# Bringing a largest value and a count to all partitions: through DRAM and VectorE, or through TensorE

## The chip, the cores and the metric

The kernel runs on one core of a Trainium2 chip. The core has TensorE (PE, matrix products and transposes into PSUM), VectorE (DVE), ScalarE (ACT), GpSimd (POOL) and SyncE (SP), which here only issues transfers. Each engine works through its own list of instructions in order; an instruction that waits holds up all that stand behind it on its engine. The metric is the device time of one execution in microseconds (us), the median of several runs.

## The reference

Two layers over x of 2 x 512 rows of 512 numbers, each an attention-like part and a feed-forward part, each followed by a layer norm. What matters here is the feed-forward part of the first layer:

```python
def _L0_ffn_ref(x, w_gate, w_up, w_down):
    xf = x / 128.0
    gate = einsum('bsh,ih->bsi', xf, w_gate)
    up = einsum('bsh,ih->bsi', xf, w_up)
    inter = silu(gate) * up
    inter_q = trunc(clip(inter * 128.0, -128.0, 127.0))
    down = einsum('bsi,hi->bsh', inter_q, w_down)
    return trunc(clip(down * 128.0, -128.0, 127.0))
```

The weights that the inputs bring are ternary: each is -s, 0 or s, with one s for each of the three matrices. The gate and up matrices are 1376 x 512, down is 512 x 1376.

## The kernel before

**Ternary weights found at run time.** The kernel doesn't take it for granted that the weights are ternary. It takes the largest weight of a first block as s, divides every weight by s, multiplies back and counts the places where the product differs from the weight. Where the count is zero, the products run on the divided weights in fp32r (a faster matmul form); if not, a branch takes the plain fp32 weights. This is done twice: "up" for gate and up together (two scales, 22 blocks to check), and "down" (one scale, 11 blocks).

A largest value or a count comes out of DVE as one number on each of 128 partitions. All partitions then need the largest over the 128, or the sum over the 128. Before the change TensorE does this:

- `over_partitions` (L180): PE transposes mx (128 x k) into PSUM as pmx (k x 128), DVE takes the maximum along the row (top) and puts it on the diagonal of a k x k tile (dg).
- `scales` (L191): PE multiplies a block of ones with dg, which gives the k values on all partitions (pbc); DVE limits them to sc and takes the reciprocal inv.
- `verdict` (L213): PE multiplies a 128 x 128 block of ones with the counts tot, so that every partition has the sum (pf); DVE turns it into yes and no, the flag (an integer on one partition, which PE reads for its branch) and eff, the scale that later steps use.

That makes six small steps on PE: pmx, pbc and pf, each for up and for down.

**Stages.** In the first stage (up to about 72 us) PE computes the queries of eight heads for each of two halves b of the rows (`queries`, L352; tiles pq). ACT takes two functions of each (e and r), and DVE joins them (q). In the turn of the second half, weight products are folded into mw (`fold`, L385: a product pmw on PE, col and mw on ACT), and `largest` (L172) takes mx_up from the first chunk of gate and up weights, gus[0]. In the turns of later heads `check_up` (L439) checks blocks: ACT divides (t, L433), DVE compares and counts (junk, L204). In the second stage (72 to 131 us) PE multiplies the queries with mw (`read`, L392; tiles po), eight row tiles after one another; ACT and DVE take the results out of PSUM, POOL adds. The last checks, the total and the verdict of up lie in this stage, and `divided` (L506) makes the divided weights tu. In the third stage (131 to 210 us) `up` (L560) runs 22 groups of products pg and pu under the branch. Beside it run mx_down, the checks of the down weights (POOL divides into td at L435, DVE compares), the total of down and its verdict (L702 to L708). The products of down (pd, L622) follow, under the second branch, and then the second layer.

**Loads and order.** SP issues nearly all loads in one queue: x and the query weights, then `wo` (16 of 512 KB, the last of which wait for free buffers), gus[0] in front of the last four, then ten more gu chunks and the small weights of the second layer (L309 to L315). The down weights wait for the room of the first stage's tiles. The gate and up weights of the second layer (L744) go into the buffers of the first layer's chunks, and each waits for the last product that reads the old chunk. A scheduler orders each engine's instructions except POOL's by the order of the program and by when it reckons that their operands are ready; `tc.issue_after(ins)` sets an instruction behind `ins` on the same engine.

Of the kernel before, what the change touches and what calls it, by code (L numbers as in the profile page):

```python
# [10 lines left out]
F32 = mybir.dt.float32  # L11
# [25 lines left out]
def kernel(  # L37
# [19 lines left out]
    nc = tc.nc  # L57
# [5 lines left out]
    xp = ctx.enter_context(tc.tile_pool(name="xp", bufs=8))  # L63
    xtp = ctx.enter_context(tc.tile_pool(name="xtp", bufs=2))
    small = ctx.enter_context(tc.tile_pool(name="small", bufs=4))
    ps = ctx.enter_context(tc.tile_pool(name="ps", bufs=8, space=PSUM))

# [11 lines left out]
    def psum(name):  # L79
        return ps.tile([P, 512], F32, tag="mm", name=name)  # L80
# [91 lines left out]
    def largest(blocks, name):  # L172

        k = len(blocks)
        mx = small.tile([P, k], F32, tag=f"mx{k}", name=f"mx_{name}", bufs=1)
        for i, w in enumerate(blocks):
            nc.vector.reduce_max(mx[:, i : i + 1], w, AX.X)
        return mx

    def over_partitions(mx, name):  # L180

        k = mx.shape[-1]
        pm = psum(f"pmx_{name}")
        nc.tensor.transpose(pm[:k, :P], mx, ident)
        top = small.tile([k, 1], F32, tag=f"top{k}", name=f"top_{name}", bufs=1)
        nc.vector.reduce_max(top, pm[:k, :P], AX.X)
        dg = small.tile([k, k], F32, tag=f"dg{k}", name=f"dg_{name}", bufs=1)
        nc.vector.tensor_scalar_mul(dg, ident[:k, :k], top)
        return dg

    def scales(dg, name):  # L191

        k = dg.shape[-1]
        pb = psum(f"pbc_{name}")
        nc.tensor.matmul(pb[:, :k], ones[:k, :], dg, start=True, stop=True)
        sc = const.tile([P, k], F32, tag=f"sc_{name}", name=f"sc_{name}")
        nc.vector.tensor_scalar(sc, pb[:, :k], 1e-30, 3e38, ALU.max, ALU.min)
        inv = const.tile([P, k], F32, tag=f"inv_{name}", name=f"inv_{name}")
        nc.vector.reciprocal(inv, sc)  # L199
        return sc, inv  # L200
# [7 lines left out]
    def total(counts, name):  # L208
        tot = small.tile([P, 1], F32, tag="tot", name=f"tot_{name}", bufs=1)
        nc.vector.reduce_sum(tot, counts, AX.X)  # L210
        return tot

    def verdict(tot, sc, name):  # L213

        k = sc.shape[-1]
        pf = psum(f"pf_{name}")
        nc.tensor.matmul(pf[:, :1], ones, tot, start=True, stop=True)
        yes = small.tile([P, 1], F32, tag="yes", name=f"yes_{name}", bufs=1)
        nc.vector.tensor_scalar(yes, pf[:, :1], 0.0, None, ALU.is_equal)
        no = small.tile([P, 1], F32, tag="no", name=f"no_{name}", bufs=1)  # L220
        nc.vector.tensor_scalar(no, pf[:, :1], 0.0, None, ALU.not_equal)
# [9 lines left out]
    def up_weights(gu_in, name, chunks=range(len(CHUNKS))):  # L231
        gus = []
        for c in chunks:
            i, n = CHUNKS[c]
            gu = wffn.tile([P, 2, NK, n], F32, tag=f"gu{c}", name=f"gu{name}_{c}")
            at = 2 * HID * i
            nc.sync.dma_start(
                gu.rearrange("p a k i -> p (a k i)"),
                gu_in[at : at + 2 * HID * n].rearrange("(p f) -> p f", p=P),
            )  # L240
            gus.append(gu)
        return gus
# [38 lines left out]
    with tc.tile_pool(name="a0w", bufs=1) as a0w, tc.tile_pool(name="a0", bufs=2) as a0:  # L281
# [24 lines left out]
                halves.append(w)  # L306
            wos.append(halves)

        gus += up_weights(gu0_in, "0", range(1, len(CHUNKS)))  # L309
        nc.sync.dma_start(wqkv, wqkv_in.rearrange("(k p) f -> p k f", p=P))  # L310
        bqk = const.tile([D, 3], F32, tag="bqk", name="bqk")
        nc.sync.dma_start(bqk, bqk_in)
        nc.sync.dma_start(bv, bv_in.to_broadcast([P, D]))
        nc.sync.dma_start(wo1, wo1_in)
        nc.sync.dma_start(bo, bo_in.to_broadcast([P, HID]))  # L315

# [24 lines left out]
        def first_queries(pq, xt):  # L341
# [7 lines left out]
                    done = query_products(pq, xt, 0, ts(t, P))  # L349
            return done  # L350

        def queries(b, xt, h):  # L352
# [8 lines left out]
            nc.scalar.activation(e, pq, AF.Exp, bias=bq[:, h : h + 1])  # L361
            r = a0.tile([D, S], F32, tag="r", name=f"r_{b}_{h}")
            nc.scalar.activation(r, pq, AF.Relu, bias=bq[:, h : h + 1])
            q = a0.tile([D, S], F32, tag="q", name=f"q_{b}_{h}", bufs=16)
            nc.vector.scalar_tensor_tensor(q, e, 1.0, r, ALU.min, ALU.add)
            qs[b].append(q)
            return done

# [97 lines left out]
        for h in range(NH):  # L466
            queries(1, xt1, h)
            if h == 0:
                sum_weights(nc.vector, 4)
                sum_weights(nc.gpsimd, 5)  # L470
                fold(0)
                fold(1)
                mx_up = largest(
                    [gus[0][:, a].rearrange("p k i -> p (k i)") for a in range(2)], "up"
                )
            elif h == 1:
                top_up = over_partitions(mx_up, "up")
            elif h == 2:
                sc_up, inv_up = scales(top_up, "up")
                fold(2)  # L480
                fold(3)
                sum_weights(nc.vector, 6)
                sum_weights(nc.gpsimd, 7)
            elif h == 3:
                fold(4)
            elif h == 5:
                fold(5)
                fold(6)
            elif h == 6:
                fold(7)  # L490
            if h >= 3:
                for _ in range(3):
                    check_up(*checks.pop(0))
        order = [(b, t) for b in range(B) for t in range(NT)]
        def norm_a0(i, steps):

# [19 lines left out]
        for i, (b, t) in enumerate(order):  # L516
            steps = read(b, t, lambda steps: norm_a0(i - 1, steps) if i else None)
            for _ in range((3, 2, 2, 0, 0, 0, 0, 0)[i]):
                check_up(*checks.pop(0))
            if i == 3:  # L520
                tot_up = total(counts, "up")
            elif i == 4:
                flag_up, eff_up = verdict(tot_up, sc_up, "up")
            if i in (3, 4, 5):
                for a in range(2):
                    divided(i - 3, a)
            if i == 5:
# [22 lines left out]
    with tc.tile_pool(name="f0", bufs=2) as f0:  # L550
# [131 lines left out]
        step = up(0, 3)  # L682
        with tc.issue_after(step.ins):
            mx_d = largest([wds[0]], "down")
        for c in range(3):
            up(1, c)
        top_d = over_partitions(mx_d, "down")
        for c in range(4, 8):
            up(0, c)
            if c == 4:  # L690
                sc_d, inv_d = scales(top_d, "down")
            up(1, c - 1)
            for i in range(2 * c - 8, 2 * c - 6):
                check_down(i)
# [4 lines left out]
        up(0, 9)  # L699
        check_down(10)  # L700
        up(0, 10)
        tot_d = total(counts_d, "down")  # L702
        up(1, 8)
        flag_d, eff_d = verdict(tot_d, sc_d, "down")
        down_scale = const.tile([P, 1], F32, tag="down_scale", name="down_scale")
        nc.vector.tensor_scalar(down_scale, eff_d, -128.0, None, ALU.mult)
        up(1, 9)
# [573 lines left out]
```

## Time and profile before

| | |
|---|---|
| median of 3 runs | 471.82 us (471.29 to 472.02) |
| the profiled execution | 471.99 us |
| its span | 470.0 us |
| TensorE clock granted | 0.996 of full speed |
| loaded and stored by transfers | 33.97 MB |

The span goes from the first to the last instruction of the profile; some 2 us of the execution lie around it. The page cuts the span into 40 slices of 11.75 us and gives the busy share of each engine in tenths:

```profile
PE   9999999999999999999999999999999999999995
DVE  1265677767857677755988989986666767998633
ACT  3344799557556877645756743575644768532201
POOL 0343101566460090400348032000000000041101
DMA  8999800000015000213192000000000000001011
```

The transfers are dense in the first five slices, up to about 57 us, and sparse after that. ACT has its fullest slices in the fifth to the seventh, where the checks of up begin. The waits that the profile lists for the six small steps are these: DVE waited 3.1 us for pmx_up, 1.9 for pbc_up, 0.6 for pf_up, 0.6 for pmx_down, 1.2 for pbc_down and 2.5 for pf_down, each once. mx_up ran at 34.8 us, inv_up at 50.2, the first check at 51.1; tot_up ended at 83.8, and the branch of up was read at 129.3. mx_down ran at 150.7, inv_down at 163.1, tot_down at 201.4, and the branch of down was read at 207.2.

### The profile page before, as it was taken

The numbers are of one execution on the slowest core, as the hardware profiler recorded it, in microseconds if no ns is written. First come the engines' busy times: TensorE is split into PE (matmuls) and PEld (weight loads), VectorE is DVE, ScalarE is ACT, GpSimd is POOL, SyncE is SP. The second block draws the span as 40 slices with busy tenths as digits, with TensorE's granted clock in tenths as the row PEclk, the third lists the DMA queues.
The fourth block names the chain that finished last, engine by engine and source line by source line (L and its number), as shares of the span: only waits on it lengthen the run. The fifth ranks groups of instructions, "written<-read, shape, count | busy, mean of one in ns | idle before, by whom it ended". The sixth has DMA issues, their size and how long they took to land.

```text
span 470.0 us, 5725 instructions
## 1 busy us (share of the span) xinstructions
PE 463.0 (99%) x1899; PEld 330.7 (70%) x1899; DVE 327.9 (70%) x622; ACT 268.1 (57%) x507; POOL 114.4 (24%) x141
## 2 busy tenths in 40 slices
PE   9999999999999999999999999999999999999995
PEld 8454444434478788888866568888888888888885
DVE  1265677767857677755988989986666767998633
ACT  3344799557556877645756743575644768532201
POOL 0343101566460090400348032000000000041101
PEclk9999999999999999999999999999999999999998
DMA  8999800000015000213192000000000000001011
GB/s 311 373 348 382 301 2 0 0 0 3 1 54 188 3 1 1 92 47 81 58 360 94 0 1 1 1 0 1 1 0 1 0 1 1 1 24 45 22 46 45
DMA packets 15187, 33.97 MB, mean 72 GB/s; under 512 B 3440, under 2 KB 4336, under 8 KB 15152
## 3 DMA queue, kind: packets, MB, share of 16 engines
q1 hardware_dynamic: 14864, 33.14, 19.6%
q8 instruction: 22, 0.36, 0.3%
q10 hardware_dynamic: 288, 0.36, 0.2%
q14 instruction: 13, 0.11, 0.1%
HBM read 31.40 MB, written 2.10 MB: 71 GB/s over the span
## 4 chain that ended last, share of the span: by engine, by line
PE 72%; ACT 7%; DVE 5%; issue 3%; POOL 0%; POOLq 0%; DVEq 0%; ACTq 0%
PE pm L1071 17%; PE pg_f L567 9%; PE pu_f L567 8%; PE pc L1071 8%; PE pdm L1159 7%; PE pd_f L622 4%; PE pdc L1159 4%; DVE x L423 4%; PE pqk L853 3%; PE po L401 2%; ACT y L414 2%; ACT t L433 2%; PE pv L866 2%; PE pot L949 1%; PE po L965 1%
## 5 line engine op out<-in xcount | busy, mean ns | idle before, releaser
L401 PE MATMUL po<-mw,q 128*128 128x512 f32 x128 | 57.1, 598 | 0.3 <-DVE mv_a L137 0.2
L325 PE MATMUL pq<-xt_a,wq 128*128 128x512 f32 (+1 forms) x152 | 56.9, 526 | 0.0
L143 POOL TENSOR_TENSOR rstd_f<-mv_f,ln_eps 128x1 f32<-128x1 f32 x15 | 4.4, 295 | 172.1 <-DVE mv_f L1174 130.2
L401 PEld LDWEIGHTS po<-mw,q 128*128 128x128 f32 x128 | 23.0, 189 | 32.1 <-issue 17.7
L325 PEld LDWEIGHTS pq<-xt_a,wq 128*128 128x128 f32 x152 | 26.2, 190 | 27.3 <-issue 26.2
L1071 PE MATMUL pm<-r,ugu 128*128 128x512 f32 x152 | 37.7, 389 | 0.0
L1071 PE MATMUL pm<-r,it_early 128*128 128x512 f32 x144 | 36.7, 392 | 0.0
L1071 PEld LDWEIGHTS pm<-r,ugu 128*128 128x128 f32 x152 | 28.5, 188 | 5.9
L1071 PEld LDWEIGHTS pm<-r,it_early 128*128 128x128 f32 x144 | 27.0, 188 | 6.0 <-issue 0.5
L423 DVE SCALAR_TENSOR_TENSOR x<-po,den,x 128x511 f32<-128x511 f32 x40 | 29.8, 745 | 1.9
L165 ACT ACTIVATE ta_f<-y_f,below_half 128x512 int8<-128x512 f32 (+1 forms) x22 | 15.9, 723 | 23.7 <-DVE y_f L155 23.3
L1081 DVE SCALAR_TENSOR_TENSOR ev_q<-pm,ev_q 128x512 f32<-128x512 f32 x27 | 18.6, 687 | 14.1 <-PE pm L1071 14.1
L418 POOL TENSOR_TENSOR y<-y,y 128x511 f32<-128x511 f32 x16 | 20.3, 1272 | 31.5 <-ACT y L414 30.8
L593 DVE SCALAR_TENSOR_TENSOR it_f<-tb_f,ta_f 128x512 fp32r<-128x512 int16 (+1 forms) x22 | 15.2, 690 | 16.3 <-ACT tb_f L166 16.3
L361 ACT ACTIVATE e<-pq,bq 128x512 f32<-128x512 f32 x16 | 11.1, 691 | 24.1 <-PE pq L325 21.7
L567 PE MATMUL pg_f<-xh,tu 128*128 128x512 f32 x88 | 24.7, 401 | 0.0
L1080 ACT ACTIVATE ev_q<-pc 128x512 f32<-128x512 f32 x27 | 16.0, 594 | 14.1 <-PE pc L1071 14.0
L435 POOL TENSOR_SCALAR td<-wd,inv_down 128x512 fp32r<-128x512 f32 x11 | 18.6, 1710 | 22.0 <-DVE inv_down L199 22.0
L567 PE MATMUL pg_f<-xl,tu 128*128 128x512 f32 x88 | 23.6, 390 | 0.0
L567 PE MATMUL pu_f<-xh,tu 128*128 128x512 f32 x88 | 23.6, 389 | 0.0
L567 PE MATMUL pu_f<-xl,tu 128*128 128x512 f32 x88 | 23.5, 389 | 0.0
L961 ACT ACTIVATE x<-x,off_f,rstd_f 128x512 f32<-128x512 f32 x7 | 5.7, 816 | 27.7 <-POOL off_f L960 27.7
(310 smaller groups left out, 1088.3 us busy)
## 6 DMA issues: line engine op xcount, KB each, us to landing
gu<-in_gu SPq DMA_DIRECT2D x20, 512.0 KB, 8.0
wo<-in_wo SPq DMA_DIRECT2D x16, 512.0 KB, 5.7
wd<-in_wd SPq DMA_DIRECT2D x20, 256.0 KB, 4.9
wq<-in_wq SPq DMA_DIRECT2D x8, 256.0 KB, 4.1
x<-in_x SPq DMA_DIRECT2D x7, 256.0 KB, 4.4
out<-x SPq DMA_DIRECT2D x7, 256.0 KB, 2.0
wqkv<-in_wqkv SPq DMA_DIRECT2D x1, 768.0 KB, 10.7
m<-in_m SPq DMA_DIRECT2D x1, 512.0 KB, 5.8
```

The lines of the kernel that those rows point to most:

```text
L165: nc.scalar.activation(a[:n], y, AF.Relu, bias=below_half[:n])
L325: done = nc.tensor.matmul(pq[:, at], wq[h][:, k, :], xt[:, k, at], start=(k == 0), stop=(k == NK - 1),)
L401: nc.tensor.matmul(po, qs[b][h0 + j][:, ts(t, P)], mw[:, h0 + j, :], start=True, stop=True,)
L418: nc.gpsimd.tensor_add(ys[0][:, :LAST], ys[0][:, :LAST], y[:, :LAST])
L423: steps.append(nc.vector.scalar_tensor_tensor(x[:, :LAST], four[j][:, :LAST], d, x[:, :LAST], ALU.mult, ALU.add))
L435: eng.tensor_scalar(out, w, factor, None, ALU.mult)
L567: nc.tensor.matmul(pp[a], t[:, a, i % NK, :], x2[b][i], start=(i == 0), stop=(i == 2 * NK - 1),)
L622: nc.tensor.matmul(pd, inter[b][c][:, ts(t, P)], td[c].bitcast(F32R), start=(c == 0), stop=(c == last),)
L1071: nc.tensor.matmul(p, w, x, start=(left[id(p)] == begun[id(p)]), stop=(left[id(p)] == 1))
L1080: nc.scalar.activation(ev, pc, AF.Copy, scale=CROSS)
L1081: nc.vector.scalar_tensor_tensor(ev, pm, MAIN, ev, ALU.mult, ALU.add)
L1159: nc.tensor.matmul(p[:, :w], got[j // 4][1][kind][:, j % 4], down_parts[j][kind][:, cols], start=(j == 0 and kind == kinds[0]), stop=(j == ...
```

## The change

The six small PE steps go. In place of `over_partitions` a function `spread` writes the 128 x k tile to DRAM in one transfer, and reads it back in a second one, as one row of 128 x k numbers that goes to every partition. DVE then takes the largest (in `scales`) or the sum (in `verdict`) along that row on every partition. The write is issued by SP; the read by ACT for the largest weights of up, and by SP in the three other places.

With it go changes of order. mx_up is set behind the last copy of the transposed rows (`copies[-1]`). The loads of the ten gu chunks and of the small weights (`later_loads`) are set behind the write of mx_up. `scales` of up is set behind an earlier query step on DVE, the checks and the first divisions behind a relu on ACT, `scales` of down behind a step of `up`. The verdict of up is called at i == 5 rather than at i == 4. The row of up takes a buffer of the tag "t", which the checks use too; that of down has a tile of its own. A tile `fill` changes its pool.

```diff
+    fill = small.tile([P, 24], F32, tag="fill", name="fill_small", bufs=1)
+    nc.gpsimd.memset(fill[0:1, 0:1], 0.0)
     ps = ctx.enter_context(tc.tile_pool(name="ps", bufs=8, space=PSUM))
+    dram = ctx.enter_context(tc.tile_pool(name="dram", bufs=1, space=bass.MemoryType.DRAM))
...
-    def over_partitions(mx, name):
-
-        k = mx.shape[-1]
-        pm = psum(f"pmx_{name}")
-        nc.tensor.transpose(pm[:k, :P], mx, ident)
-        top = small.tile([k, 1], F32, tag=f"top{k}", name=f"top_{name}", bufs=1)
-        nc.vector.reduce_max(top, pm[:k, :P], AX.X)
-        dg = small.tile([k, k], F32, tag=f"dg{k}", name=f"dg_{name}", bufs=1)
-        nc.vector.tensor_scalar_mul(dg, ident[:k, :k], top)
-        return dg
-
-    def scales(dg, name):
-
-        k = dg.shape[-1]
-        pb = psum(f"pbc_{name}")
-        nc.tensor.matmul(pb[:, :k], ones[:k, :], dg, start=True, stop=True)
+    sent = []
+
+    def spread(part, room, name, queues):
+
+        k = part.shape[-1]
+        there = dram.tile([P, k], F32, name=f"held_{name}")
+        sent.append(queues[0].dma_start(there, part))
+        every = room[:, : k * P]
+        queues[1].dma_start(
+            every, there.rearrange("(o p) k -> o (p k)", o=1).to_broadcast([P, k * P])
+        )
+        return every.rearrange("q (p k) -> q k p", k=k)
+
+    def scales(every, name):
+
+        k = every.shape[1]
         sc = const.tile([P, k], F32, tag=f"sc_{name}", name=f"sc_{name}")
-        nc.vector.tensor_scalar(sc, pb[:, :k], 1e-30, 3e38, ALU.max, ALU.min)
+        nc.vector.reduce_max(sc, every, AX.X)
+        nc.vector.tensor_scalar(sc, sc, 1e-30, 3e38, ALU.max, ALU.min)
...
-    def verdict(tot, sc, name):
+    def verdict(every, sc, name):
...
-        pf = psum(f"pf_{name}")
-        nc.tensor.matmul(pf[:, :1], ones, tot, start=True, stop=True)
+        pf = small.tile([P, 1], F32, tag="pf", name=f"pf_{name}", bufs=1)
+        nc.vector.reduce_sum(pf, every[:, 0, :], AX.X)
...
-                mx_up = largest(
-                    [gus[0][:, a].rearrange("p k i -> p (k i)") for a in range(2)], "up"
-                )
-            elif h == 1:
-                top_up = over_partitions(mx_up, "up")
+                with tc.issue_after(copies[-1].ins):
+                    mx_up = largest(
+                        [gus[0][:, a].rearrange("p k i -> p (k i)") for a in range(2)], "up"
+                    )
+                room = a0.tile([P, NK * P], F32, tag="t", name="t_mx")
+                every_up = spread(mx_up, room, "mx_up", (nc.sync, nc.scalar))
+                with tc.issue_after(sent[-1].ins):
+                    later_loads()
             elif h == 2:
-                sc_up, inv_up = scales(top_up, "up")
+                with tc.issue_after(elus[-2].ins):
+                    sc_up, inv_up = scales(every_up, "up")
...
                 for _ in range(3):
-                    check_up(*checks.pop(0))
+                    with tc.issue_after(relus[NH + 2].ins):
+                        check_up(*checks.pop(0))
...
             if i == 3:
-                tot_up = total(counts, "up")
-            elif i == 4:
-                flag_up, eff_up = verdict(tot_up, sc_up, "up")
+                room = a0.tile([P, NK * P], F32, tag="t", name="t_tot")
+                every_up = spread(total(counts, "up"), room, "tot_up", (nc.sync, nc.sync))
+            elif i == 5:
+                flag_up, eff_up = verdict(every_up, sc_up, "up")
             if i in (3, 4, 5):
                 for a in range(2):
-                    divided(i - 3, a)
+                    with tc.issue_after(relus[NH + 3].ins):
+                        divided(i - 3, a)
...
             mx_d = largest([wds[0]], "down")
+        room = f0.tile([P, P], F32, tag="every", name="every_mx", bufs=1)
+        every_d = spread(mx_d, room, "mx_d", (nc.sync, nc.sync))
         for c in range(3):
-            up(1, c)
-        top_d = over_partitions(mx_d, "down")
+            before, step = step, up(1, c)
         for c in range(4, 8):
             up(0, c)
             if c == 4:
-                sc_d, inv_d = scales(top_d, "down")
+                with tc.issue_after(before.ins):
+                    sc_d, inv_d = scales(every_d, "down")
...
         up(0, 10)
-        tot_d = total(counts_d, "down")
+        room = f0.tile([P, P], F32, tag="every", name="every_tot", bufs=1)
+        every_d = spread(total(counts_d, "down"), room, "tot_d", (nc.sync, nc.sync))
         up(1, 8)
-        flag_d, eff_d = verdict(tot_d, sc_d, "down")
+        flag_d, eff_d = verdict(every_d, sc_d, "down")
```

More of the change, by code (lines that the diff above doesn't have):

```diff
@@ L211, in total @@
         return tot
-    def verdict(tot, sc, name):
+    def verdict(every, sc, name):
         k = sc.shape[-1]
-        pf = psum(f"pf_{name}")
-        nc.tensor.matmul(pf[:, :1], ones, tot, start=True, stop=True)
+        pf = small.tile([P, 1], F32, tag="pf", name=f"pf_{name}", bufs=1)
+        nc.vector.reduce_sum(pf, every[:, 0, :], AX.X)
         yes = small.tile([P, 1], F32, tag="yes", name=f"yes_{name}", bufs=1)
-        nc.vector.tensor_scalar(yes, pf[:, :1], 0.0, None, ALU.is_equal)
+        nc.vector.tensor_scalar(yes, pf, 0.0, None, ALU.is_equal)
         no = small.tile([P, 1], F32, tag="no", name=f"no_{name}", bufs=1)
-        nc.vector.tensor_scalar(no, pf[:, :1], 0.0, None, ALU.not_equal)
+        nc.vector.tensor_scalar(no, pf, 0.0, None, ALU.not_equal)
         flag = const.tile([1, 1], I32, tag=f"flag_{name}", name=f"flag_{name}")
@@ L307, with later_loads @@
             wos.append(halves)
-        gus += up_weights(gu0_in, "0", range(1, len(CHUNKS)))
-        nc.sync.dma_start(wqkv, wqkv_in.rearrange("(k p) f -> p k f", p=P))
         bqk = const.tile([D, 3], F32, tag="bqk", name="bqk")
[L312 to L315, printed above, removed]
+        def later_loads():
+            gus.extend(up_weights(gu0_in, "0", range(1, len(CHUNKS))))
+            nc.sync.dma_start(wqkv, wqkv_in.rearrange("(k p) f -> p k f", p=P))
+            nc.sync.dma_start(bqk, bqk_in)
+            nc.sync.dma_start(bv, bv_in.to_broadcast([P, D]))
+            nc.sync.dma_start(wo1, wo1_in)
+            nc.sync.dma_start(bo, bo_in.to_broadcast([P, HID]))
         mw = a0w.tile([D, NH, HID], F32, tag="mw", name="mw")
@@ L350, in first_queries @@
             return done
+        relus, elus = [], []
         def queries(b, xt, h):
@@ L362, in queries @@
             r = a0.tile([D, S], F32, tag="r", name=f"r_{b}_{h}")
-            nc.scalar.activation(r, pq, AF.Relu, bias=bq[:, h : h + 1])
+            relus.append(nc.scalar.activation(r, pq, AF.Relu, bias=bq[:, h : h + 1]))
             q = a0.tile([D, S], F32, tag="q", name=f"q_{b}_{h}", bufs=16)
-            nc.vector.scalar_tensor_tensor(q, e, 1.0, r, ALU.min, ALU.add)
+            elus.append(nc.vector.scalar_tensor_tensor(q, e, 1.0, r, ALU.min, ALU.add))
             qs[b].append(q)
```

## The prediction, made before the run

> **What bounds the kernel now.** First the page's busy shares: TensorE (PE) is the only engine without idle time, so an instruction taken from it can be worth its whole slot, and another engine's work costs only where it makes PE wait.
>
> ```profile
> PE 463.0 (99%) x1899; PEld 330.7 (70%) x1899; DVE 327.9 (70%) x622; ACT 268.1 (57%) x507; POOL 114.4 (24%) x141
> ```
>
> Matmul ends are modelled, so next I read PE's timeline by starts. An fp32 128x512 matmul starts every 0.43 us, and a group of four f32r ones every 0.905 us (151.34, 152.24, 153.15, 154.06). What the small matmuls cost is how far they push these starts apart. PE's timeline in two windows, the six of them being pmx, pbc, pf of "up" and of "down" (up's first two here):
>
> ```profile
> 44.66 1.45 PE L325 MATMUL pq<-xt_a,wq 128*128 128x512 f32 x3
> 45.95 0.27 PE L184 MATMUL pmx_up<-ident,mx_up 128*2 128x128 f32 x1
> 46.06 1.45 PE L325 MATMUL pq<-xt_a,wq 128*128 128x512 f32 x3
> ...
> 48.63 1.02 PE L325 MATMUL pq<-xt_a,wq 128*128 128x512 f32 x2
> 49.59 0.38 PE L195 MATMUL pbc_up<-dg_up,ones 2*128 2x2 f32 x2
> 49.89 1.98 PE L387 MATMUL pmw<-wos,m 128*128 128x512 f32 x4
> ```
>
> and the "down" ones, in the same view of later windows:
>
> ```profile
> 161.46 1.07 PE L567 MATMUL pu_f<-xl,tu 128*128 128x512 f32 x4
> 162.46 0.38 PE L195 MATMUL pbc_down<-dg_down,ones 1*128 1x1 f32 x2
> 162.77 1.21 PE L567 MATMUL pg_f<-xh,tu 128*128 128x512 f32 x4
> 163.82 1.09 PE L567 MATMUL pg_f<-xl,tu 128*128 128x512 f32 x4
> ...
> 205.56 1.07 PE L567 MATMUL pu_f<-xl,tu 128*128 128x512 f32 x4
> 206.46 0.28 PE L217 MATMUL pf_down<-tot_down,ones 128*128 128x1 f32 x2
> 206.60 1.17 PE L567 MATMUL pg_f<-xh,tu 128*128 128x512 f32 x4
> 207.61 1.07 PE L567 MATMUL pg_f<-xl,tu 128*128 128x512 f32 x4
> ```
>
> Then the chain of waits: from 131 us on nearly every piece of it is PE (the pieces around pbc_down: pu_f 0.68, pbc_down 0.31, pg_f 1.38). Between 55 and 119 us it runs through ACT and DVE. There ACT is what to look at (its timeline):
>
> ```profile
> 49.69 0.69 ACT L361 ACTIVATE e<-pq,bq 128x512 f32<-128x512 f32 x1 [2.28 <-PE pq L325]
> 50.28 0.68 ACT L363 ACTIVATE r<-pq,bq 128x512 f32<-128x512 f32 x1
> 51.06 0.17 ACT L389 ACTIVATE col<-pmw 128x1 f32<-128x1 f32 x1
> 51.12 0.72 ACT L433 ACTIVATE t<-gu,inv_up 128x512 fp32r<-128x512 f32 x1
> ```
>
> The reader should see that ACT still waits for PE at 49.69, and that its first check starts at 51.12, about 0.75 us after inv_up is there (50.20 + 0.17). From there to 83 us ACT has less than 1 us of idle time. So the largest weights have 0.75 us of slack before they delay a full engine. Last, the loads: ten gu loads are issued from 36.39 on (SP's timeline), and the page's DMA issues have what each took to land. Late on, SP holds loads back until PE has done with their buffers; these two come next to the down verdict:
>
> ```profile
> 206.70 0.33 SPq L237 DMA_DIRECT2D gu<-in_gu  x1
> ...
> 210.59 0.33 SPq L237 DMA_DIRECT2D gu<-in_gu  x1
> ```
>
> **What the Trainium skill says.** "DMA: Bandwidth & Descriptors", section "Two DMAs through the same engine are not ordered": a transfer that reads what another wrote must wait at its issuing engine for the first one's completion. Each hop is thus two full transfers end to end, and the issuing queue stands still between; no earlier transfer here reads what another wrote. Its "Latency and other measured facts" gives about 0.8 us as least for a tiny transfer; the trace's shortest median is 1.8 us (160 KB of output), so I use the trace. Its "Queues, rings and completion order" has each DMA engine take turns between queue rows, so a read issued by ACT should not stand behind all of SP's loads. The one load on ACT's queue, 256 KB of x at the start, landed in 3.5 us; bqk and bv, behind the gu loads on SP, took 9.6 and 8.6 us. This agrees, but the starts differ in load. "VectorE: DVE Perf Modes", "The perf-mode tier table", has tensor_reduce at its lowest rate everywhere; the trace has 0.68 us for 512 elements and 0.28 us for 128, and I interpolate 0.41 us for 256.
>
> **The change, part by part.**
>
> *Removed from PE.* Spacing with the small matmul, less the undisturbed spacing: pmx_up 46.06 - 44.66 - 3 x 0.43 = 0.11; pbc_up 49.89 - 48.63 - 2 x 0.43 = 0.40; pf_up 107.76 - 106.33 - 3 x 0.43 = 0.14; pmx_down 159.63 - 157.68 - 2 x 0.905 = 0.14; pbc_down 163.82 - 161.46 - 1.81 = 0.55; pf_down 207.61 - 205.56 - 1.81 = 0.24. Down: 0.93 us. Up: 0.65 us. Down lies where PE alone sets the end, so all 0.93 is gained if nothing new is late. Up lies ahead of the stretch where ACT is full: only what brings ACT's checks forward counts. That is 0.11 (pmx_up lies ahead of the pq that ACT waits for at 49.69) and 0.21, since r ends at 50.85 and col waits until 51.06 for a fold that is now 0.40 earlier. Together 0.32. pf_up lies where PE already waits for ACT (the y at 105.86): 0, at most 0.14.
>
> *Added on DVE.* Up: 0.41 + 0.16 + 0.17 us in place of 0.28 + 0.22 + 0.16 + 0.17; down about even; each verdict gains a sum over 128 elements, 0.28 us, and loses its wait for PE (0.63 and 2.47 us). The up verdict goes from the fifth to the sixth read tile, where transposes make PE the bound. Cost 0; from -0.6 (the lost wait, if DVE is the chain at 107.9) to +0.5 (about 0.9 us of verdict less the slack PE leaves there). DVE idles about 27% of 107-131 us and 31% of 200-235.
>
> *Largest weights of up.* DVE now takes mx_up behind the last copy of xt (37.83 at the latest), and behind a weight sum of 1.21: done by 37.83 + 1.21 + 1.28 = 40.3 at worst; near 37.9 if the 1.23 + 1.28 us that mx_up took at 34.75 go away ahead of it. I take 37.9. SP's write of 1 KB, with wo loads ahead of it in its queue, lands in about the wo row's 5.8 us: 43.7. ACT issues the read (0.41 us, as its issue of x) and waits for it to be allowed; behind it queue e(1,0), two folds and e(1,1). ACT idles 2.3 us before 46.15 and 2.28 before 49.69, so a wait to 43.7 is hidden; were it three us longer, 0.5 would show. Read in 3.5 us: lands at 47.6, ahead of q(1,1) at 47.45-48.1, which the scale is tied behind. inv_up at 48.9, not 50.4. Bounds: 2 us if idle, 8.6 us if it stands in line like bv.
>
> *Later loads.* Ten gu loads and five small ones move behind that write: from 36.39 to about 38. SP issued a 512 KB gu in some 0.87 us while they took 9.5 us to land, so the DMA engines have work in hand and lose at most 1 us. Chunk 1 is needed near 54 and its load then lands near 47: 0.
>
> *Largest of down.* mx_d at 151.4; write and read of 2 to 2.7 us each with SP free (its next load is at 188.56): lands by 157. inv_down comes near 158.5 instead of 163.2; POOL starts early, nobody gains: 0.
>
> *Mismatches of down.* tot_down ends 201.57. Write 2.0, issue 0.4, read 2.0 to 2.7: 206.0 to 206.7, sum 0.28: near 206.8, as yes_down now (206.78). Behind it on DVE wait the it and y of up. PE needs the flag ahead of 210.34; it now takes 0.32 us to load at 207.2, with about 0.6 us of branching. Slack some 2 us: 0. Mismatches of up have 20 us: 0.
>
> *Sum.* -0.93 - 0.32 = -1.25 us. Profiled execution 471.99 (span 470.0 and 1.99 around it): 470.7. The median is 0.17 lower: 470.6. Its own range is 469.6 (all 1.58 and the DVE wait of 0.6) to 471.4 (0.93 less 0.5).
>
> **The rivals.** What a measurement here can tell from none is 0.2%, 0.94 us.
>
> *Slower, A: the largest weights of up come late.* If the read stands behind the gu loads like bv, it lands at 44.1 + 8.6 = 52.7, inv_up at 53.5, and checks that would start near 50.8 start 2.7 us late on an engine with no idle time to catch up; PE then waits at the po matmuls, where it already waits for ACT at 79 us. -1.04 (0.93 and pmx_up) + 2.7 = +1.7: 473.5. It decides from a landing past about 52.1 (2.0 us late). For: the DMA is over 90% busy until 57 us, a new ACT wait, 8-byte rows. Against: a queue of its own.
>
> *Slower, B: the down verdict gets in line behind weights.* SP keeps its order. If the load that waits for PE until 210.59 is placed ahead of tot_down's read, the flag comes near 214 and PE stands still some 4.6 us: 475.1. Behind the 206.70 load only, 0.7 us are lost. For: SP is shared. Against: tot_down is ready 5 us before the 206.70 load.
>
> *No change: hidden anyway.* The up gain is lost to shifted orders and a late transfer of a microsecond eats part of down's: 471.4.
>
> **How the numbers follow.** Forecast 0.50 (0.42 over the bound, 0.08 within it); no change 0.18; A 0.22 and B 0.10, of which 0.02 ends within the bound. Faster 0.42, same 0.28, slower 0.30. Predicted 470.6. The range goes from 469.6 to 473.8, which takes in A at its price and leaves out its worse half and B.
>
> **What would show it.** PE's starts at 157-164 and 205-208 evenly 0.905 apart; inv_up before 50.4; no new idle on ACT after 51; the every_up read landing within about 4 us; the down flag by 208. A first check after 52, PE idle ahead of the down matmuls, or a longer wait of po for ACT would make the prediction wrong.

## The result, and the profile after

The change made the kernel slower: 492.17 us in the median of five runs (491.15 to 494.39), against 471.68 us for the kernel before beside it. The ratio is 1.0429, with a 95% interval of 1.0412 to 1.0446. The profiled execution took 491.15 us, its span 489.2 us, 19.2 more than before.

The page of the changed kernel, its busy shares and two rows of the 40 slices (12.2 us each):

```profile
PE 464.5 (95%) x1889; PEld 332.3 (68%) x1889; DVE 326.5 (67%) x622; ACT 267.8 (55%) x507; POOL 113.8 (23%) x142
...
PE   9999999499999999973999999999999999999995
...
PEclk9999999799999999995999999999999999999999
```

PE has about as much work as before, 464.5 us, but 95% in place of 99%: two holes, in the eighth slice (86 to 98 us) and around the nineteenth (217 to 230 us). In both places the granted clock falls too (7 and 5 tenths in the row PEclk). PE's timeline of the changed kernel at the two holes (start, duration, instruction, and in brackets the idle time before it and what ended it):

```profile
93.87 13.47 PE L409 MATMUL po<-mw,q 128*128 128x512 f32 x26 [6.62 <-DVE yes_up L223]
...
227.90 6.79 PE L637 MATMUL pd_f<-td,it_f 128*128 128x512 f32 x22 [10.86 <-DVE eff_down L229]
```

Both end with a verdict on DVE. DVE's timeline says what the verdicts waited for:

```profile
85.02 0.17 DVE L417 RECIPROCAL den<-den 128x4 f32<-128x4 f32 x1
92.88 0.29 DVE L221 TENSOR_REDUCE pf_up<-t_tot 128x1 f32<-128x128 f32 x1 [7.68 <-DMA t_tot<-held_tot_up]
93.08 0.74 DVE L431 SCALAR_TENSOR_TENSOR x<-po,den,x 128x511 f32<-128x511 f32 x1
...
171.65 0.29 DVE L200 TENSOR_REDUCE sc_down<-every_mx 128x1 f32<-128x128 f32 x1 [6.29 <-DMA every_mx<-held_mx_d]
...
212.72 0.17 DVE L214 TENSOR_REDUCE tot_down<-counts_d 128x1 f32<-128x11 f32 x1
...
226.17 0.29 DVE L221 TENSOR_REDUCE pf_down<-every_tot 128x1 f32<-128x128 f32 x1 [8.73 <-DMA every_tot<-held_tot_d]
```

All three waits end with the landing of a transfer. The first is in the second read tile (85 us), though the program calls the verdict at i == 5, in the sixth: the scheduler set pf_up there on DVE. Behind it stands x, the step that takes a product po out of PSUM, and the next po started at 93.87, when x had ended (93.08 + 0.74). The profile names yes_up as what released it, but po doesn't read yes_up, which ended at 93.88, after that start. The chain of waits of the changed kernel puts the last stretch in order (start, length, what):

```profile
212.91 7.51 DMA held_tot_d<-tot_down
...
220.47 5.67 DMA every_tot<-held_tot_d
...
227.90 6.79 PE pd_f L637 x22
```

And the page's DMA issues have the landing time of each small transfer (last column, us):

```profile
t_mx<-held_mx_up ACTq DMA_DIRECT2D x1, 128.0 KB, 7.5
...
t_tot<-held_tot_up SPq DMA_DIRECT2D x1, 64.0 KB, 4.9
every_mx<-held_mx_d SPq DMA_DIRECT2D x1, 64.0 KB, 4.4
every_tot<-held_tot_d SPq DMA_DIRECT2D x1, 64.0 KB, 5.7
...
held_mx_up<-mx_up SPq DMA_DIRECT2D x1, 1.0 KB, 6.1
...
held_tot_up<-tot_up SPq DMA_DIRECT2D x1, 0.5 KB, 7.9
held_mx_d<-mx_down SPq DMA_DIRECT2D x1, 0.5 KB, 8.3
held_tot_d<-tot_down SPq DMA_DIRECT2D x1, 0.5 KB, 7.5
```

Half a KB takes 7.5 to 8.3 us to be written, with the DMA engines nearly idle beside it (a busy share of 0.01 to 0.03 in those three stretches). That is longer than the 512 KB loads of wo took in the same run (6.9 us).

The starts of the stages on PE give the account. First po: 72.31 before, 71.70 after (-0.61). First pg: 130.65 and 138.18, so the read stage grew by 8.14 us; 6.62 of it is the hole. First pd: 210.34 and 227.90, so the stage of up grew by 10.03; that is the hole of 10.86 less the 0.93 that PE was spared, and 0.1. First pqk of the second layer: 235.8 and 255.0, another 1.6. Sum 19.2. What is left beside the holes shows in the windows of the changed kernel (stretch, its length, then busy us and instructions of PE, PEld, DVE, ACT and POOL, the granted clock, the DMA share and GB/s):

```profile
86.00:94.00 8.00, 1.38 (x4) 0.51 (x3) 1.12 (x6) 2.00 (x7) 3.04 (x3) 0.82 0.03 8
94.00:98.20 4.20, 4.20 (x6) 1.75 (x7) 3.94 (x10) 0.52 (x2) 0.74 (x2) 0.52 0.00 0
217.00:228.00 11.00, 0.14 (x2) 0.13 (x1) 2.23 (x9) 0.29 (x1) 0.00 (x0) 0.68 0.24 98
228.00:234.60 6.60, 6.60 (x23) 5.30 (x24) 2.89 (x7) 3.82 (x6) 0.00 (x0) 0.76 0.02 8
```

After the first hole PE runs for 4.2 us at a clock of 0.52 and does 6 products; before the change the same stretch held 10 at 1.00. That is another 4 x 0.43 = 1.7 us. After the second hole the clock is 0.76 over 6.6 us, which costs 0.24 x 6.6 = 1.6 us. The Trainium skill, "TensorE: Matmul & The Clock Gate", section "What's actually happening", says that after an idle window of about 3.4 us the array runs at half its clock and needs about as long a busy stretch to get back. The two holes, of 6.6 and 10.9 us, agree with it; where the limit lies no run here shows.

### The profile page after: what moved, and what is told of

The parts are those of the page before. It is cut to its first block, busy times and chain, and to the rows that moved or that the text cites. A ratio compares the mean times of both kernels' runs of the same rounds, so it can differ in the third digit from the quotient of the medians.

```text
span 489.2 us, 5731 instructions
## 1 busy us (share of the span) xinstructions
PE 464.5 (95%) x1889; PEld 332.3 (68%) x1889; DVE 326.5 (67%) x622; ACT 267.8 (55%) x507; POOL 113.8 (23%) x142
## 4 chain that ended last, share of the span: by engine, by line
PE 51%; DMA 3%; issue 2%; DVE 1%; POOL 0%; POOLq 0%; ACT 0%; SPq 0%
PE pm L1089 16%; PE pc L1089 8%; PE pdm L1177 7%; PE pd_f L637 4%; PE pdc L1177 4%; PE pqk L871 3%; DMA held_tot_d<-tot_down 2%; PE pv L884 1%; PE pot L967 1%; PE po L983 1%; PE psc L909 1%; DMA every_tot<-held_tot_d 1%; PE pt_a L128 1%; PE pt_f L1020 1%; PE pt_p L128 1%
## 5 line engine op out<-in xcount | busy, mean ns | idle before, releaser
L409 PE MATMUL po<-mw,q 128*128 128x512 f32 x128 | 58.4, 612 | 7.2 <-DVE yes_up L223 6.6
L409 PEld LDWEIGHTS po<-mw,q 128*128 128x128 f32 x128 | 24.4, 196 | 39.6 <-issue 22.0
L637 PE MATMUL pd_f<-td,it_f 128*128 128x512 f32 x88 | 21.9, 411 | 10.9 <-DVE eff_down L229 10.9
L637 PEld LDWEIGHTS pd_f<-td,it_f 128*128 128x128 f32 x88 | 17.6, 201 | 15.0 <-issue 11.3
L413 ACT ACTIVATE den<-po,den_eps 128x1 f32<-128x1 f32 x64 | 14.9, 275 | 22.9 <-PE po L409 22.9
L369 ACT ACTIVATE e<-pq,bq 128x512 f32<-128x512 f32 x16 | 11.1, 692 | 24.1 <-PE pq L331 19.2
```

The lines of the kernel that those rows point to most:

```text
L409: nc.tensor.matmul(po, qs[b][h0 + j][:, ts(t, P)], mw[:, h0 + j, :], start=True, stop=True,)
L637: nc.tensor.matmul(pd, inter[b][c][:, ts(t, P)], td[c].bitcast(F32R), start=(c == 0), stop=(c == last),)
```

## The experiments

Theory 1: the loss is the time of the round trips (write to DRAM and read back), and of two things it meets: the verdict of up stands too early on DVE, and the verdict of down has too little room. Rival: the new orders of work cost it, and the transfers only show where. A second question is why half a KB takes 8 us. The kernel before, run beside these kernels, had medians of 471.97 to 472.01 us; ratios are against it.

### The price of the transfers

```diff
# the kernel before, behind tot_up, all on SP
...
+                d1 = dram.tile([P, 1], F32, name="d_small")
+                d2 = dram.tile([P, P], F32, name="d_apart")
+                d3 = dram.tile([P, P], F32, name="d_wide")
+                row = d1.rearrange("(o p) k -> o (p k)", o=1)
+                nc.sync.dma_start(d1, tot_up)
+                nc.sync.dma_start(t1, row.to_broadcast([P, P]))
+                nc.sync.dma_start(d3, t1)
+                nc.sync.dma_start(t3, d3)
+                nc.sync.dma_start(d2[:, 0:1], t3[:, 0:1])
+                nc.sync.dma_start(s2, d2[:, 0:1])
+                nc.sync.dma_start(s4, s2)
+                d5 = dram.tile([1, P], F32, name="d_row")
+                nc.sync.dma_start(d5, s4)
+                nc.sync.dma_start(t4, d5.to_broadcast([P, P]))
```

t1, t3, t4 and s2 are parts of one tile t_a in SBUF; s4 is a row on one partition (s_e in the profile).

> The kernel before, with nine transfers more that no engine but SP waits for, one after another from tot_up (83.8 us) on, while the DMA engines are idle. Theory 1 (each row of 4 bytes is a small write of its own, and the rows of one DMA engine follow one another): the 4-byte rows packed together in DRAM land in 7.5 to 8.3 us as in the changed kernel, the 4-byte rows 512 bytes apart in the same 7 to 8 us, rows of 512 bytes in 2 to 3 us, one row of 512 bytes in about 2 us. Theory 2 (the packed rows collide in one stretch of DRAM): packed 7.5 to 8.3, apart 2 to 3. Theory 3 (any write to DRAM is that slow): 512-byte rows take over 6 us too. Reads: the row that goes to all partitions in 4.4 to 5.7 us, 512-byte rows of their own in 2 to 3 if reading one place 128 times is what costs, the same 4 to 6 if not. SBUF to SBUF, 4-byte rows: about 2 us if the slowness is DRAM's, 7 if it is that of small rows. Time of the kernel: as before, 471 to 473 us, by all theories; more if the transfers by themselves disturb the others.

471.76 us in one run, in the midst of the kernel before (471.13 to 473.38): the transfers alone cost the kernel nothing that shows. Its DMA issues (d_small: 4-byte rows packed, which means side by side without a gap; d_apart: 4-byte rows 512 bytes apart; d_wide: rows of 512 bytes; s_e: one row on one partition):

```profile
t_a<-d_small SPq DMA_DIRECT2D x1, 64.0 KB, 4.8
d_wide<-t_a SPq DMA_DIRECT2D x1, 64.0 KB, 1.5
...
t_a<-d_row SPq DMA_DIRECT2D x1, 64.0 KB, 2.8
...
d_small<-tot_up SPq DMA_DIRECT2D x1, 0.5 KB, 7.7
d_apart<-t_a SPq DMA_DIRECT2D x1, 0.5 KB, 1.4
...
s_e<-t_a SPq DMA_DIRECT2D x1, 0.5 KB, 2.0
```

The same 128 values of 4 bytes land in 1.4 us when they lie 512 bytes apart and in 7.7 us when they are packed. It is neither the size of the rows nor their number that costs, but where they lie: theory 2. A second run asked how near is too near:

```diff
# the kernel before, behind tot_up; (spacing in words, words in a row)
+                shapes = ((16, 1), (8, 1), (4, 1), (2, 1), (4, 4), (16, 16))
+                for n, (step, width) in enumerate(shapes):
+                    d = dram.tile([P, step], F32, name=f"w{step}x{width}_")
+                    part = src[:, 32 * n : 32 * n + width] if n else tot_up
+                    nc.sync.dma_start(d[:, :width], part)
...
# and behind mx_down
...
+        nc.sync.dma_start(ds, mx_d)
+        for _ in range(2):
+            nc.sync.dma_start(every, ds.rearrange("(o p) k -> o (p k)", o=1).to_broadcast([P, P]))
+        nc.sync.dma_start(dw, every)
+        for _ in range(2):
+            nc.sync.dma_start(every, dw[0:1, :].to_broadcast([P, P]))
```

> The kernel before, with measuring transfers that nothing reads afterwards, all on SP and each waiting for the one ahead. From tot_up on: 128 rows written to DRAM with 4 bytes each, 64, 32, 16 and 8 bytes apart (w16x1, w8x1, w4x1, w2x1), then packed rows of 16 bytes (w4x4) and of 64 bytes (w16x16), each read back into 128 partitions. From mx_down on: packed 4-byte rows (ds_packed) with the broadcast read twice in a row, then a 64 KB write (dw_wide) and the broadcast read of its first 512 bytes twice. Theory A (the cost comes from rows that fall into one small block of DRAM, 64 bytes or so): 64 bytes apart 1.4-2.0 us as with 512 bytes apart, 32 and 16 bytes apart in between, 8 bytes apart 4-8 us; packed 16-byte rows 3-5 us, packed 64-byte rows 1.4-2.0 us. Theory B (the cost comes from rows that fall into one stretch of 512 bytes or more): 64 bytes apart already 2.5-4 us or more, packed 64-byte rows likewise. For the broadcast read: if the read just after the packed write pays for the packed write (rows still on their way), the first takes 4.5-5.7 us and the second 2.8 us; if a read of 128 times the same 512 bytes costs that by the weight of traffic beside it, both take the same, and the reads of dw_wide take as long. The kernel itself ends at 471-473 us.

472.53 us in one run. Its DMA issues, four of the writes (the number behind w is the spacing in words of 4 bytes; w4x__851 has rows of four words, the other two w rows of one):

```profile
w4x__845<-t_a SPq DMA_DIRECT2D x1, 0.5 KB, 1.4
...
w2x__848<-t_a SPq DMA_DIRECT2D x1, 0.5 KB, 3.2
...
w4x__851<-t_a SPq DMA_DIRECT2D x1, 2.0 KB, 1.4
...
ds_packed<-mx_down SPq DMA_DIRECT2D x1, 0.5 KB, 7.8
```

16 bytes apart, the rows land in 1.4 us (so do those at 32 and 64 bytes); 8 bytes apart 3.2; packed 7.8. Rows of 16 bytes that touch each other take 1.4 too, and rows of 64. Theory A was right in kind, and its block was too large: rows that start 16 bytes apart cost nothing more, rows that start 8 bytes apart do. Theory B fell. The Trainium skill, "DMA: Bandwidth & Descriptors", section "Specifications", says that below 512 bytes a transfer engine reads, modifies and writes; here that alone costs nothing that shows, since 4-byte rows landed in 1.4 us and rows of 512 bytes in 1.5. The first broadcast read after the packed write took 4.7 us, the second 2.8. After the wide write the two reads of a row of 512 bytes took 3.1 and 2.9, so 1.6 to 1.9 us of the first read come from the packed write before it. What the memory does with packed rows these runs do not show.

### The two places

```diff
# run 1, against the changed kernel
-                flag_up, eff_up = verdict(every_up, sc_up, "up")
+                with tc.issue_after(steps[-1].ins):
+                    flag_up, eff_up = verdict(every_up, sc_up, "up")
# run 2, against the changed kernel
-        room = f0.tile([P, P], F32, tag="every", name="every_tot", bufs=1)
-        every_d = spread(total(counts_d, "down"), room, "tot_d", (nc.sync, nc.sync))
+        tot_d = total(counts_d, "down")
...
-        flag_d, eff_d = verdict(every_d, sc_d, "down")
+        flag_d, eff_d = verdict_pe(tot_d, sc_d, "down")
```

`verdict_pe` is the verdict of the kernel before, with its sum by TensorE. Run 3 has both edits.

> The changed kernel with the verdict of up tied behind the last DVE step of the sixth read tile, so that it is late enough for its transfers. Theory 1 (DVE stands still behind a transfer that is not there yet, PE runs out of PSUM buffers, then runs at half clock for some 4 us): no DVE wait for t_tot, PE idle at po falls from 7.2 to under 1 us, and the time falls by 6.6 + 2, to 483 to 484 us. Theory 2 (the new order of loads and checks costs it, not this wait): 490 to 492 us.

> The changed kernel with the mismatches of down summed by TensorE as before; the three other places stay with the transfers. Theory 1: PE's 10.9 us idle ahead of pd and the 1.6 us of low clock behind it go, as tot_down (212.7) is 4 us ahead of PE's end of the up products (216.9): 479 to 480 us. Theory 2 (the late start of the down checks is what holds the flag up, not its two transfers): tot_down is still late, and 485 us or more remain.

> Both edits at once: two of the six PE steps of before are back at most (pf of down), the verdict of up waits late. Theory 1: the two stalls are all of the loss, 471 to 472 us, since five of the six small PE steps are gone (about 1.3 us) and some of that is given back by the DVE wait of 6.3 us for the scale of down. Theory 2: if order and loads cost by themselves, 475 us or more.

Run 1 took 484.63 us (ratio 1.0270, 1.0250 to 1.0291), 7.5 less than the changed kernel; run 2 478.55 us (1.0142, 1.0115 to 1.0168), 13.6 less; run 3 472.14 us (0.9996, 0.9980 to 1.0012), 20.0 less. All three lie within 0.7 us of the ranges of theory 1 and far from those of theory 2. The two places make the whole loss. In run 1 DVE's timeline has no wait left at pf_up, and the one at pf_down as before:

```profile
120.81 0.28 DVE L221 TENSOR_REDUCE pf_up<-t_tot 128x1 f32<-128x128 f32 x1
...
219.25 0.28 DVE L221 TENSOR_REDUCE pf_down<-every_tot 128x1 f32<-128x128 f32 x1 [8.86 <-DMA every_tot<-held_tot_d]
```

In run 1 tot_down started at 205.68, 4.3 us later than before the change, as DVE had waited 6.7 us for every_mx. Had it been on time, its round trip of 13.4 us would still have ended near 215, and pd was due near 209.4 (210.34 less 0.93).

Run 3 gained nothing over the kernel before, though PE was spared five of its six steps. Its times scatter from 470.2 to 473.4. In its profiled execution (473.3 us, one of the longest of the twelve) ACT's timeline shows where the gain went:

```profile
45.54 0.69 ACT L380 ACTIVATE e<-pq,bq 128x512 f32<-128x512 f32 x1 [6.98 <-DMA held_mx_up<-mx_up]
...
53.82 0.72 ACT L452 ACTIVATE t<-gu,inv_up 128x512 fp32r<-128x512 f32 x1 [3.07 <-DVE inv_up L203]
```

The largest weights of up are late there, the first check of ACT starts at 53.8 in place of 51.1, and the read stage takes 61.0 us in place of 58.3. This is the prediction's rival A, with its price of 2.7 us (inv_up at 53.6, where it reckoned 53.5). In the profiled execution of run 1 the check started at 51.1, and that stage took 58.7. That this difference makes the scatter of run 3 is not shown, as only one of its executions has a profile.

### The round trip alone

```diff
# against the changed kernel, in the three places on SP
-        room = f0.tile([P, P], F32, tag="every", name="every_tot", bufs=1)
-        every_d = spread(total(counts_d, "down"), room, "tot_d", (nc.sync, nc.sync))
+        room = f0.tile([P, 2 * P], F32, tag="every", name="every_tot", bufs=1)
+        every_d = spread_row(total(counts_d, "down"), room, "tot_d")
...
# spread_row: 128 partitions -> one row on one partition -> one row in DRAM -> all partitions
+        row, every = room[0:1, P : 2 * P], room[:, :P]
+        there = dram.tile([1, P], F32, name=f"held_{name}")
+        nc.sync.dma_start(row, part)
+        nc.sync.dma_start(there, row)
+        nc.sync.dma_start(every, there.to_broadcast([P, P]))
...
```

> The changed kernel with one thing altered: in the three places on SP (tot_up, mx_down, tot_down) the 128 values first go from 128 partitions into one row on one partition (2.0 us measured), that row of 512 bytes goes to DRAM (about 1.1) and is read by all partitions (2.8): about 6.5 us with the issues, in place of 12.6 to 13.6. The place of the verdict of up on VectorE stays where the scheduler puts it. Theory (the length of the round trip is the cause): TensorE's wait before the verdict of up falls from 6.6 us to under 1.5, the wait of sc_down to under 1, the idle stretch before pd from 10.9 us to 0-4; 471.5 to 475 us. Rival (the place in the order is the cause, and VectorE loses the same whatever the transfer takes): 480 us or more, with the waits of the changed kernel.

471.97 us in 20 runs (0.9996, 0.9983 to 1.0008): 20.2 us came back with no step of the program moved, and one transfer more in each place. SP's timeline, and DVE's line of the verdict of down:

```profile
201.75 0.48 SPq L200 DMA_DIRECT2D every_tot<-tot_down  x1
203.66 0.24 SPq L201 DMA_DIRECT2D held_tot_d<-every_tot  x1
204.79 0.32 SPq L202 DMA_DIRECT2D every_tot<-held_tot_d  x1
```

```profile
208.03 0.28 DVE L230 TENSOR_REDUCE pf_down<-every_tot 128x1 f32<-128x128 f32 x1
```

The first two of the three transfers (hops) take 1.91 and 1.13 us from issue to next issue, and the last landed in 2.8; pf_down no longer waits. pf_up still stands in the second read tile, at 86.6 us, and waits for nothing. The scheduler itself set pf_up behind one x more, and pf_down behind one y more, than in the changed kernel; these steps take some 0.7 and 1.1 us, not the 7.7 and 8.7 that DVE had waited. So the place of that verdict costs only because the row came late; the rival falls. What this kernel doesn't gain goes to ACT again, which waited 2.0 us for inv_up, as the largest weights of up still go packed: its stage of up is 1.0 us shorter than before the change, its read stage 1.6 longer.

### Leaving out the late largest weights, and a surprise

Two more kernels held the verdict of up, gave the largest weights of up back to TensorE and put the loads in their old order; one has the three hops for down, the other the verdict of down by TensorE.

> The three hops of the run beside it, with the verdict of up held behind the last product of its read tile, and the largest weights of up by TensorE with the loads in their old order. Against the kernel before, TensorE is spared pf_up (0.14 us), pmx_down, pbc_down and pf_down (0.93) and nothing should wait: 470.5 to 471.3 us, if the loss before pd is gone; if the round trip of 6.5 us still ends after the last product of up, VectorE's work before pd is 2 to 4 us late and the time is 472.5 to 475.

> The changed kernel with the verdict of up held, the mismatches of down summed up by TensorE, and the largest weights of up by TensorE with the loads in their old order: only the mismatches of up and the largest weights of down go by DRAM, with 12 to 13 us each. By theory both are hidden here: TensorE is spared pf_up, pmx_down and pbc_down (0.14 + 0.14 + 0.55 = 0.83 us), so 470.7 to 471.5 us, and the times scatter less than the 470.2 to 473.4 of the run with both repairs, since ScalarE no longer waits for held_mx_up. Rival (the scatter there has another cause): 471 to 472.5 with the same scatter of 3 us.

Both missed: 476.20 us (1.0084, 1.0072 to 1.0097) and 476.50 us (1.0092, 1.0079 to 1.0106). No engine showed a new wait of that size. But most groups of products of 512 columns in fp32r took 392 to 394 ns (pm from r and ugu, in the second layer, 393 in the mean, 389 in the kernel before); those in fp32 stayed at 592. The cause suspected was the addresses. The change doesn't move the tile `fill` to another pool, as the part on the change has it: the old one stays, and a second, `fill_small`, comes to the small pool. Its 96 bytes and the 32 of the new pf make up for four tiles of 32 bytes that the change takes out of that pool (top and dg, for up and down). With the two for up back beside `fill_small`, all later tiles lay 64 bytes further. Four runs tested that:

```diff
# in the two kernels
-    fill = small.tile([P, 24], F32, tag="fill", name="fill_small", bufs=1)
+    fill = small.tile([P, 8], F32, tag="fill", name="fill_small", bufs=1)
# the kernel before
+    fill = small.tile([P, 16], F32, tag="fill", name="fill_small", bufs=1)
+    nc.gpsimd.memset(fill[0:1, 0:1], 0.0)
# the changed kernel
-    fill = small.tile([P, 24], F32, tag="fill", name="fill_small", bufs=1)
-    nc.gpsimd.memset(fill[0:1, 0:1], 0.0)
```

> The three hops with the verdict of up held and the largest weights of up by TensorE, as in the run that took 476.2 us, with the filling tile in the small pool cut from 24 to 8 columns (96 to 32 bytes), so that the two tiles that TensorE's way takes there (top and dg, 32 bytes each by the pool's steps) move no later tile. There, the products of 512 columns took 392-394 ns in the mean in place of 389. Theory (the tiles behind the small pool lay 64 bytes further, and that made the products slower): 389 ns again, about 4 us less: 471.0 to 472.3 us. Rival (the orders of work cost it): the products stay at 392-394 ns and the time at 475.5 to 477.

> The same cut of the filling tile in the run that took 476.5 us (mismatches of down and largest weights of up by TensorE). Theory of the addresses: 471.0 to 472.3 us and 389 ns. Rival: 475.5 to 477.

> The kernel before with one tile of 64 bytes per partition added at the head of its small pool and one value set in it by GpSimd; nothing else. It moves every later tile by 64 bytes. Theory of the addresses: products of 512 columns at 392-394 ns and 475.5 to 477 us. Rival (addresses don't matter): 389 ns and 471.4 to 472.2 us.

> The changed kernel without its filling tile (96 bytes per partition) in the small pool; nothing else. The tiles behind it lie 96 bytes lower than in the kernel before. Theory of the addresses, if any shift that is no multiple of 128 bytes does it: 392-394 ns and some 4 us more than the changed kernel: 495.5 to 497.5 us. If only some shifts do it, or none: 491 to 493.5 us and 389 ns.

471.06 us (0.9983, 0.9976 to 0.9990), 472.13 us (1.0002, 0.9993 to 1.0011), 476.73 us (1.0103, 1.0087 to 1.0118) and 496.10 us (1.0520, 1.0504 to 1.0536). In the kernel before with 64 bytes more and no other change, the groups by line on PE read (busy us, mean ns, idle before):

```profile
L1073 PE MATMUL pm<-r,ugu 128*128 128x512 f32 x152 | 38.3, 393 | 0.0
...
L624 PE MATMUL pd_f<-td,it_f 128*128 128x512 f32 x88 | 20.8, 394 | 0.0
```

Unmoved, both have 389. The 1,191 products of this kind in the profile (352 of up, 88 of down, the rest in the second layer), some 3.8 ns longer each, make 4.6 us, and the run lost 4.7. The tile `fill_small` of the change thus earns its place: without it (the fourth run, all later tiles 96 bytes lower, pm at 395 ns) the changed kernel takes 3.9 us more. Which tiles have to stay where they were, and why, was not tried.

The three hops with the held verdict are the best kernel of the case, 0.95 us below the kernel before: at the border of what can be told, with an interval that leaves out 1, and close to the 1.07 us (0.14 and 0.93) that PE is spared in it by the prediction's account. The other one gains nothing. Its largest weights of down still go packed, DVE is some 5 us late with tot_down, and PE waits for it (PE's timeline in its profiled execution, 473.1 us):

```profile
206.82 0.35 PE L243 MATMUL pf_down<-tot_down,ones 128*128 128x1 f32 x2 [0.47 <-DVE tot_down L236]
```

## Why the prediction was wrong

It said 470.6 us and at most 473.8; 492.2 came. One term carries most of the miss.

- *"Mismatches of down": "Write 2.0, issue 0.4, read 2.0 to 2.7 ... Slack some 2 us: 0."* This is the step that failed. The write took 7.5 and the read 5.7. The round trip was 13.2 us where 4.4 to 5.1 were reckoned, and neither the range nor a rival held that case. The prices were taken from the trace's shortest transfers (160 and 256 KB of output in 1.8 to 2.0 us), as if bytes were what counts; a write of 4-byte rows side by side was not in that trace. The prediction names 8-byte rows as a point for rival A, but gives them no price. Of its own signs of being wrong, PE idle ahead of the down products is the one that came. With a round trip of 6.3 us (three hops) the step holds as reasoned: the verdict is there at 208.0 and costs nothing. The run with the sum back on TensorE puts this place at 13.6 us.
- *"Largest of down ... lands by 157 ... nobody gains: 0."* The same price: 8.3 and 4.4 us. DVE waited 6.3 us for it with its other work queued behind, and of the 11.3 us by which tot_down was late, 7.5 came from the read stage and 3.8 from here. It is no hole of its own, but it feeds the one before pd.
- *"Mismatches of up have 20 us: 0", with "The up verdict goes from the fifth to the sixth read tile".* Two faults met: the scheduler set the verdict in the second tile, presumably because it reckoned the row ready there (no view shows its reckoning), and the round trip of 12.9 us ended 7.7 us too late for that. Held behind its tile's last step it costs nothing, as reckoned (7.5 us came back); with the short round trip it costs nothing in the early place either.
- *What a hole costs beyond itself* was left out: 1.6 to 1.7 us of low clock after each.
- *Right: what PE was spared.* For down 0.93 us was reckoned; the stage accounts agree to 0.1. For up 0.32 us was reckoned ahead of ACT's checks, and col on ACT did come 0.32 us earlier (50.74 for 51.06), but the first check behind it then waited for inv_up. (The prediction has r end at 50.85; by its line r ends at 50.96, 50.28 + 0.68. The size came out all the same.) The first po came 0.61 us earlier, but this says little: the kernels with TensorE's way for these weights have it anywhere from 71.7 to 73.6 us, those with the transfers at 71.4 to 71.7.
- *Right with a wrong part: "Largest weights of up".* The write landed in 6.1 us, close to the 5.8 taken, but that may be luck: 5.8 is the time of a 512 KB load, and this was 1 KB in 8-byte rows side by side. The wait of ACT for it, to 43.70, was hidden as reckoned. The read took 7.5 us, not 3.5, although it had ACT's queue to itself; bv, half as large, took 7.9 on SP's. How much of it came from the loads and how much from the packed write before it these runs do not separate. The first check of ACT came at 51.68, 0.6 us later than before. Rival A named a late read, and run 3 shows its price.
- *Rival B*, the verdict behind weight loads in SP's queue, did not come about: in the changed kernel and in the one with three hops both transfers of tot_down are issued ahead of the loads in question.

## What to carry to other kernels

Price a small transfer by how its rows lie, not by its bytes: values from 128 partitions that end up side by side in DRAM cost 6 us more than the same values 16 bytes apart, and the next read pays some 2 us too. Making one row of them in SBUF first cured it here; to leave them 16 bytes apart in DRAM and read them so to all partitions was not tried. Before a step is costed at nothing because it has room, find where the scheduler will put it on its engine, for an instruction that waits holds up all behind it. When a small tile is added to or taken from a pool, compare the mean durations of products far away from it.

## What the runs showed of the hardware that was not expected

- 128 rows of 4 bytes to DRAM: 7.5 to 8.3 us packed, 3.2 at 8 bytes apart, 1.4 from 16 bytes on. The first broadcast read of 512 bytes after the packed write took 4.4 to 5.7 us, a second one 2.8; of one row of 512 bytes 2.8 to 3.5.
- From 128 partitions into one row on one partition, SBUF to SBUF: 1.9 to 2.0 us.
- Tiles 64 bytes further in SBUF, or 96 bytes lower: products of 512 columns in fp32r at 392 to 395 ns in most groups in place of 389, fp32 products unchanged at 592; 3.9 to 4.7 us in this kernel.
